# Dividing one pair's attention context by a second product's sums instead of dividing its weights first, with three small moves in the opening order

## The chip, the cores and the metric

One core of one Trainium2 chip runs the whole kernel. The time is the device time of one execution in microseconds (us); the time before is the median of three runs. The trace is of one further execution and counts from the start of its span.

## The reference, cut to what matters

`x` and `ctx_1024` are 128 batches of 128 tokens of 256 numbers, all in float32. One cross-attention block with 16 heads of 16 is followed by a feed-forward layer of 1024.

```python
q = heads(x @ Wq + bq); k = heads(ctx @ Wk + bk); v = heads(ctx @ Wv + bv)
scores = einsum('bhqd,bhkd->bhqk', q, k) / sqrt(16)
scores = where(j < i, scores, -1e30)        # query i, key j: strictly lower
attn = softmax(scores);  attn[:, :, 0, :] = 0
h = layer_norm(x + einsum('bhqk,bhkd->bhqd', attn, v) @ Wo + bo) * g1 + b1n
out = layer_norm(h + relu(h @ W1 + b1) @ W2 + b2) * g2 + b2n
```

## The kernel before

The 128 batches go through the core as 64 pairs, numbered p from 0. A pair's tokens are 256 columns of the transposed tiles `xT` and `cT`. `queries`, `keys` and `values` are products on TensorE; ScalarE (ACT) takes queries and keys out of PSUM with scale and bias. `values_out` copies the values into two tiles padded with zeros, `vz` and `vd`, and fills one half of `vd` with a DMA.

The scores of a pair come in two parts. `scores(p, 1)` has the queries 64 to 127 against 128 keys (2048 columns for the 16 heads), `scores(p, 0)` the queries 0 to 63 against 64 keys (1024 columns: the low scores). Both batches of the pair lie on the 128 partitions. For each part the softmax is a relay of four engines:

- `mask` on VectorE (DVE, L345): scores plus the mask, PSUM to the tile `sm`.
- `maximum`: a row maximum on DVE (L356), its subtraction on GpSimd (POOL, L357).
- `exponential` on ACT (L364).
- `sums`: row sums on DVE (L376), their reciprocals on DVE (L377), the multiplication of the weights by them on POOL (L378).

`ONE`, `TWO` and `ALL` are heads 0 to 7, 8 to 15, and all of them. The weights are then transposed to `pT`. In the steady stage this is done by DVE and by DMAs (`turn`, `bring`); for pairs 0, 1 and 63 it is done on TensorE, with ACT copying the transposes out of PSUM (`turn_on_pe`, L421 and L423). `weigh` multiplies `pT` with the values into one PSUM bank `pc` (96 small matmuls, L438 and L448). `context` copies `pc` into `cxT` on ACT (L460), leaving out token 0. `attention_out` (L467) applies Wo. `attention_sum`, `attention_stats` and `norm1` are DVE and POOL work that yields the normalised `x1`; for pair 0 `norm1` is L508, and TensorE transposes `x1` (L226, tile `ptn`).

Everything is under `manual_schedule` for all engines, so each engine runs its instructions in the order in which the program issues them. That order is written out by hand: first an opening for pairs 0 and 1, then `step(p)` for p = 2 to 62, then a closing for pair 63 and the rest. In `step`, pair 2 has branches of its own. TensorE's results go to PSUM tiles of two kinds: two tiles of two banks for scores (`pair`), and four single banks for everything else (`bank`).

The opening of before, where the change lies, runs in this order: transposes of pair 0, `bkh`, `bvw`, `bqs_c` (the query bias times the score scale), `queries(0)`, keys of pair 0, `scores(0, 1)`, transposes of pair 1, `values(0)`, the softmax of pair 0 mixed with `queries(1)`, `scores(0, 0)`, `keys(1)`, `values(1)`, `fold_values` and `scores(1, 1)`; then `turn_on_pe(0, ...)`, `scores(1, 0)`, `weigh(0)`, `context(0)`, `attention_out(0)`, with pair 1's softmax between them, and `queries(2)`, `keys(2)`, `values(2)`. Then `step(2)` begins with `scores(2, 1)`.

Of the kernel before, what the change touches and what calls it, by code (L numbers as in the profile page):

```python
# [8 lines left out]
F32 = mybir.dt.float32  # L9
# [4 lines left out]
P = 128  # L14
# [5 lines left out]
def tile_cross_attention_block(  # L20
# [178 lines left out]
    for i in range(2):  # L199
        vz = const.tile([P, 2, HH, 4, DK], F32, tag=f"vz{i}", name=f"vz{i}")  # L200
        nc.gpsimd.memset(vz, 0.0)
        vzs.append(vz)
        vd = const.tile([P, 2, HH, 2, DK], F32, tag=f"vd{i}", name=f"vd{i}")
        nc.gpsimd.memset(vd, 0.0)
        vds.append(vd)

    cxT = const.tile([P, KC, 2, P], F32, tag="cxT", name="cxT")
    nc.gpsimd.memset(cxT, 0.0)
# [4 lines left out]
    def bank(name):  # L213
        return ps_1.tile([P, 512], F32, tag="ps1", name=name)
# [137 lines left out]
    def maximum(p, hi, part):  # L352
        st = states[p]
        n = P if hi else HP
        sm, nmx = st["sm", hi], st["nmx", hi]
        nc.vector.tensor_reduce(nmx[:, part], sm[:, part, :], AX.X, ALU.max, negate=True)  # L356
        nc.gpsimd.tensor_tensor(  # L357
            sm[:, part, :], sm[:, part, :],
            nmx[:, part, None].to_broadcast([P, part.stop - part.start, n]), ALU.add,
        )  # L360

    def exponential(p, hi, part):
        sm = states[p]["sm", hi]
        nc.scalar.activation(sm[:, part, :], sm[:, part, :], AF.Exp)  # L364
# [3 lines left out]
    def sums(p, hi, part):  # L368

        st = states[p]  # L370
        sm = st["sm", hi]
        n = sm.shape[2]
        su = small.tile([P, H], F32, tag=f"su{hi}", name=f"su{hi}_{p}_{part.start}")
        rs = small.tile([P, H], F32, tag=f"rs{hi}", name=f"rs{hi}_{p}_{part.start}")
        su, rs = su[:, part], rs[:, part]
        nc.vector.tensor_reduce(su, sm[:, part, :], AX.X, ALU.add)  # L376
        nc.vector.reciprocal(rs, su)  # L377
        nc.gpsimd.tensor_tensor(  # L378
            sm[:, part, :], sm[:, part, :],
            rs[:, :, None].to_broadcast([P, part.stop - part.start, n]), ALU.mult,  # L380
        )
# [43 lines left out]
                pt.rearrange("p (n i a) -> p n i a", i=NS, a=32),  # L425
            )

    def weigh(p):

        st = states[p]  # L430
        pT = st.pop("pT")
        pc = bank(f"pc_{p}")

        for m in range(KC):
            for s in range(2):
                at = (m * 2 + s) * P
                for j in range(NS):
                    nc.tensor.matmul(  # L438
                        pc[32 * j : 32 * j + 32, at : at + HP],
                        st["vd"][:, s, 4 * m + j].rearrange("p e d -> p (e d)"),  # L440
                        pT[:, 2 * s : 2 * s + 2, H + 2 * j + m, :],
                        start=True, stop=True,
                    )
            for s in range(2):
                at = (m * 2 + s) * P
                for e in range(2):
                    for j in range(NS):
                        nc.tensor.matmul(  # L448
                            pc[32 * j : 32 * j + 32, at + HP : at + P],
                            st["vz"][:, s, 4 * m + j, 2 * e : 2 * e + 2, :].rearrange(  # L450
                                "p e d -> p (e d)"
                            ),
                            pT[:, 2 * s : 2 * s + 2, 4 * j + 2 * m + e, :],
                            start=(e == 0), stop=(e == 1),
                        )
        st["pc"] = pc

    def context(p):
        pc = states[p].pop("pc").rearrange("p (u i) -> p u i", i=P)
        nc.scalar.copy(cxT.rearrange("p m s i -> p (m s) i")[:, :, 1:], pc[:, :, 1:])  # L460

    def attention_out(p):
        st = states[p]
# [141 lines left out]
    def add_values(ps):  # L605
        nc.vector.scalar_tensor_tensor(bov_r, ps[:, :D], live, bo_r, ALU.mult, ALU.add)
# [78 lines left out]
    for which, first in (("x", tokens_of[0][:, 0:2]), ("c", c_first[:, 0:2])):  # L685
# [2 lines left out]
        pt = transposed(first, f"pt{which}_0")  # L688
        nc.vector.tensor_copy(st[which + "T"].rearrange("p k i -> p (k i)"), pt)  # L689

    bkh = const.tile([P, KC, 2], F32, tag="bkh", name="bkh")
    for m in range(KC):
        nc.vector.tensor_scalar(bkh[:, m, :], half, bk_c[:, m : m + 1], None, ALU.mult)

    bvw = const.tile([P, KC, P], F32, tag="bvw", name="bvw")
    nc.vector.tensor_copy(bvw, bv_c[:, :, None].to_broadcast([P, KC, P]))

    bqs_c = const.tile([P, KC], F32, tag="bqs_c", name="bqs_c")
    nc.vector.tensor_scalar(bqs_c, bq_c, QSCALE, None, ALU.mult)

    queries(0)

# [38 lines left out]
    mask(0, 0, 1)  # L741
    maximum(0, 0, ALL)
    exponential(0, 1, TWO)
    sums(0, 1, ONE)
    keys(1)
    sums(0, 1, TWO)
    exponential(0, 0, ALL)
    values(1)
    ps_bv = fold_values()
    sums(0, 0, ALL)  # L750
    scores(1, 1)
    mask(1, 1, 0)
    add_values(ps_bv)
    maximum(1, 1, ONE)
    turn_on_pe(0, 1, range(2))
    values_out(1)
    turn_on_pe(0, 1, range(2, 4))
    mask(1, 1, 1)
    maximum(1, 1, TWO)
    add_bo(0)  # L760
    turn_on_pe(0, 0, range(2))
    tokens(2, "x")
    scores(1, 0)
    exponential(1, 1, ONE)
    weigh(0)
    context(0)
    mask(1, 0, 0)
    mask(1, 0, 1)
    maximum(1, 0, ALL)
    tokens(2, "c")  # L770
    attention_out(0)
    exponential(1, 1, TWO)
    sums(1, 1, ONE)
    attention_sum(0)
    attention_stats(0)
    exponential(1, 0, ALL)
    queries(2)
    sums(1, 1, TWO)
    keys(2)
    norm1(0)  # L780
# [18 lines left out]
    def step(p):  # L799
        nonlocal waiting  # L800
        if p > 2:
            load_ahead(p)
        scores(p, 1)
        mask(p, 1, 0)
        maximum(p, 1, ONE)
        if p > 2:
            second(p - 3, 0)
            mask(p, 1, 1)
            maximum(p, 1, TWO)
            exponential(p, 1, ONE)  # L810
            second(p - 3, 1)
            if p + 2 < NP:
                tokens(p + 2, "c")
        else:
            turn_x1_on_pe(0)
            turn_on_pe(1, 1, range(2))
            fold_norm1()
            add_b1()
            hidden(0, range(FC // 2))
            mask(p, 1, 1)  # L820
            maximum(p, 1, TWO)
            exponential(p, 1, ONE)
            turn_on_pe(1, 1, range(2, 4))
            low_scores(p)
            hidden(0, range(FC // 2, 3 * FC // 4))
            turn_on_pe(1, 0, range(2))
            tokens(3, "x")
            add_bo(1)
        summed = []
        sums(p, 1, ONE)  # L830
        exponential(p, 1, TWO)
        if p > 2:
            second_sum(p - 3)
            summed = [p - 3]
        else:
            tokens(3, "c")
            load_ahead(2)
            load_tokens(2)
            exponential(p, 0, ALL)
        sums(p, 1, TWO)  # L840


        weigh(p - 1)
        context(p - 1)
        if p > 2:
            scores(p, 0)
        if p == 3:
            scale_w1()
            nc.gpsimd.tensor_tensor(b1e_c, b1e_c, b1_c, ALU.add)
        queries(p + 1)  # L850
        if p > 2:
            mask(p, 0, 0)
            mask(p, 0, 1)
            maximum(p, 0, ALL)
        if p > 2:
            exponential(p, 0, ALL)
        else:
            sums(p, 0, ALL)
            add_bo(2)
        turn(p, 1, 0)  # L860
        turn(p, 1, 1)
        for q in waiting:
            finish(q)
        attention_out(p - 1)
        attention_sum(p - 1)
        if p > 2:
            sums(p, 0, ALL)
        else:
            turn(p, 0, 0)
            bring(p, nc.sync, range(NS * NS // 2))  # L870
        attention_stats(p - 1)
        if p + 2 < NP:
            tokens(p + 2, "x")
            if p == 2:
                tokens(p + 2, "c")
        if p > 2:
            turn(p, 0, 0)
            bring(p, nc.sync, range(NS * NS // 2))
        keys(p + 1)
        norm1(p - 1)  # L880
        turn_x1(p - 1)
        values(p + 1)
        values_out(p + 1)
        for q in waiting:
            store(q)
        add_bo(p + 1)
        if p == 2:
            residual1(0)
        residual1(p - 1)
        for q in summed:  # L890
            stats(q, states[q]["t2"], 2)
        for q in summed:
            scale_and_shift(q)
        at = NS * NS // 2

        def share(f):
            nonlocal at
            n = NS * NS - at if f == FC - 2 else 0 if f == 0 or p == 2 else NS // 2
            bring(p, nc.scalar, range(at, at + n))
            at += n  # L900

        hidden(p - 2, range(0 if p > 2 else 3 * FC // 4, FC), share)
        for q in summed:
            norm2(q)
        waiting = summed
# [129 lines left out]
```

## Time and profile before

| what | value |
|---|---|
| median of three runs | 1587.98 us (1587.69 to 1590.0) |
| profiled execution, its own time | 1587.93 us |
| span of its trace | 1586.2 us |
| TensorE (PE) busy | 1572.0 us, 99% of the span |
| DVE busy | 1373.7 us, 87% |
| POOL busy | 1282.1 us, 81% |
| ACT busy | 756.7 us, 48% |
| granted TensorE clock | 1.0 |

The profiled execution lies 0.05 us below the median, and 1.73 us of it lie outside the span. A share of busy time is a mean over the opening, 61 steps and the closing. The change touches only the opening and step 2, so it is the first 75 us that have to be read instruction by instruction.

### The profile page before, as it was taken

What the parts mean: (1) busy time and instruction counts of PE and PEld (TensorE: products, weight loads), DVE (VectorE), ACT (ScalarE), POOL (GpSimd) and SP (SyncE); (2) the same over time, 40 slices, a digit from 0 to 9 for tenths busy, and PEclk for the clock granted to TensorE, in tenths of its full rate; (3) what the DMA queues carried; (4) which work ended last, traced back from release to release, by engine and by line L of the source; (5) the groups of instructions that cost most, each with busy time, mean ns of one, the idle gap of its engine ahead of it and who ended that gap; (6) DMA issues with size and microseconds to landing.
All of it is one profiled execution on the core that took longest, in us unless ns stands there. A gap on an engine that the chain in (4) does not pass through costs nothing.

```text
span 1586.2 us, 41271 instructions
## 1 busy us (share of the span) xinstructions
PE 1572.0 (99%) x16512; PEld 1329.7 (84%) x16512; DVE 1373.7 (87%) x1990; ACT 756.7 (48%) x1498; POOL 1282.1 (81%) x1104
## 2 busy tenths in 40 slices
PE   8999999999999999999999999999999999999998
PEld 6788888888888888888888888888888888888887
DVE  7999888888898888898898988888889888889872
ACT  5555445444444454454444544544444455445442
POOL 7888888788888888888888888888888888788883
PEclk9999999999999999999999999999999999999999
DMA  9555655655556556556556565565555655654521
GB/s 198 111 133 125 153 141 120 148 126 135 147 127 148 133 125 157 139 120 148 129 135 150 127 147 125 120 159 131 136 135 126 150 147 121 148 136 105 127 78 34
DMA packets 479935, 210.12 MB, mean 132 GB/s; under 512 B 348672, under 2 KB 448256, under 8 KB 479744
## 3 DMA queue, kind: packets, MB, share of 16 engines
q1 hardware_dynamic: 371104, 134.29, 38.4%
q10 hardware_dynamic: 108640, 73.19, 17.7%
q8 instruction: 131, 2.15, 0.6%
q14 instruction: 60, 0.49, 0.1%
HBM read 70.00 MB, written 33.03 MB: 65 GB/s over the span
## 4 chain that ended last, share of the span: by engine, by line
PE 95%; DMA 1%; DVE 1%; POOL 1%; issue 1%; SPq 0%; ACT 0%; ACTq 0%; POOLq 0%; DVEq 0%
PE ph L646 28%; PE py L664 27%; PE pq L260 7%; PE po L467 7%; PE pv L292 7%; PE pk L260 7%; PE pss L326 7%; PE pc L448 3%; PE pc L438 2%; DMA vd<-vz 0%; PE ptp L421 0%; POOL sm L378 0%; DMA x1t<-tbx 0%; DVE sm L345 0%; DMA c_first<-in_ctx_dram 0%
## 5 line engine op out<-in xcount | busy, mean ns | idle before, releaser
L357 POOL TENSOR_TENSOR sm<-sm,nmx 128x1024 f32<-128x1024 f32 x192 | 364.3, 1898 | 119.7 <-DVE nmx L356 119.4
L646 PE MATMUL ph<-x1T,w 128*128 128x256 f32 x2048 | 453.5, 380 | 0.3 <-DMA x1T<-x1t 0.3
L664 PE MATMUL py<-w,hT 128*128 128x256 f32 x2016 | 452.5, 383 | 0.0
L664 PEld LDWEIGHTS py<-w,hT 128*128 128x128 f32 x2016 | 378.8, 190 | 71.5 <-issue 15.0
L378 POOL TENSOR_TENSOR sm<-sm,rs 128x1024 f32<-128x1024 f32 x192 | 364.4, 1899 | 89.5 <-DVE rs L377 87.8
L646 PEld LDWEIGHTS ph<-x1T,w 128*128 128x128 f32 x2048 | 389.9, 191 | 52.9 <-DMA x1T<-x1t 0.6
L652 ACT ACTIVATE hT<-ph,b1e_c 128x256 f32<-128x256 f32 x504 | 208.4, 471 | 203.3 <-PE ph L646 103.1
L364 ACT ACTIVATE sm<-sm 128x1024 f32<-128x1024 f32 x192 | 201.4, 1054 | 206.3 <-POOL sm L357 205.7
L376 DVE TENSOR_REDUCE su<-sm 128x8 f32<-128x1024 f32 (+1 forms) x192 | 233.7, 1217 | 64.8 <-ACT sm L364 62.0
L345 DVE TENSOR_TENSOR sm<-pss,neg 128x1024 f32<-128x1024 f32 (+1 forms) x256 | 235.3, 940 | 51.5 <-PE pss L326 51.2
L391 DVE STREAM_TRANSPOSE tb<-sm 128x1024 f32<-128x1024 f32 x183 | 220.0, 1227 | 28.4 <-POOL sm L378 28.4
L356 DVE TENSOR_REDUCE nmx<-sm 128x8 f32<-128x1024 f32 (+1 forms) x192 | 234.2, 1220 | 6.6
L542 ACT ACTIVATE t<-t,nb,sd 128x256 f32<-128x256 f32 x124 | 67.7, 593 | 187.0 <-DMA pT<-tb 120.9
L260 PE MATMUL pq<-xT,wq 128*128 128x256 f32 x512 | 127.6, 392 | 0.3 <-DVE xT L689 0.3
L282 ACT ACTIVATE kT<-pk,bkh,half 128x256 f32<-128x256 f32 x252 | 120.6, 558 | 3.6 <-PE pk L260 3.6
L467 PE MATMUL po<-wo,cxT 128*128 128x256 f32 x512 | 121.1, 380 | 0.7 <-ACT cxT L460 0.7
L292 PE MATMUL pv<-wv,cT 128*128 128x256 f32 x512 | 121.0, 380 | 0.0
L260 PE MATMUL pk<-cT,wk 128*128 128x256 f32 x504 | 119.2, 380 | 0.0
L326 PE MATMUL pss<-kT,qT 32*64 32x256 f32 (+1 forms) x4096 | 116.4, 334 | 1.7 <-ACT kT L713 1.3
L271 ACT ACTIVATE qT<-pq,bqs_c 128x256 f32<-128x256 f32 x128 | 53.6, 469 | 121.5 <-PE pq L260 116.3
L260 PEld LDWEIGHTS pq<-xT,wq 128*128 128x128 f32 x512 | 92.4, 190 | 20.9 <-issue 10.3
L521 POOL TENSOR_TENSOR x1b<-x,g_r 128x512 f32<-128x512 f32 x64 | 81.7, 1277 | 34.8 <-DVE x L513 34.8
(93 smaller groups left out, 1764.1 us busy)
## 6 DMA issues: line engine op xcount, KB each, us to landing
pT<-tb SPq DMA_DIRECT2D x488, 96.0 KB, 2.9
pT<-tb ACTq DMA_DIRECT2D x488, 96.0 KB, 2.7
out_dram<-t ACTq DMA_DIRECT2D x63, 256.0 KB, 2.5
xb<-in_x_dram SPq DMA_DIRECT2D x124, 128.0 KB, 4.4
cb<-in_ctx_dram SPq DMA_DIRECT2D x124, 128.0 KB, 4.4
x<-in_x_dram SPq DMA_DIRECT2D x31, 512.0 KB, 5.5
x1t<-tbx SPq DMA_DIRECT2D x248, 64.0 KB, 2.3
x1T<-x1t SPq DMA_DIRECT2D x62, 256.0 KB, 3.2
```

Of the source, the lines that this page charges most:

```text
L260: nc.tensor.matmul(ps[:, m * TP : (m + 1) * TP], w[:, k, m * P : (m + 1) * P], src[:, k, :], start=(k == 0), stop=(k == KC - 1),)
L292: nc.tensor.matmul(pv[:, s * D : (s + 1) * D], st["cT"][:, k, s * P : (s + 1) * P], wv[:, k, :], start=(k == 0), stop=(k == KC - 1),)
L326: nc.tensor.matmul(sps[r // 2][s * HP : (s + 1) * HP, r % 2, m * 2 * n : (m + 1) * 2 * n].rearrange("p (e j) -> p e j", e=2), st["qT"][str ...
L345: nc.vector.tensor_tensor(st["sm", hi][:, part, :].rearrange("p (r n) j -> p r n j", r=2), st["sps", hi][t][:, :, : 4 * n].rearrange("p r ...
L356: nc.vector.tensor_reduce(nmx[:, part], sm[:, part, :], AX.X, ALU.max, negate=True)
L357: nc.gpsimd.tensor_tensor(sm[:, part, :], sm[:, part, :], nmx[:, part, None].to_broadcast([P, part.stop - part.start, n]), ALU.add,)
L376: nc.vector.tensor_reduce(su, sm[:, part, :], AX.X, ALU.add)
L378: nc.gpsimd.tensor_tensor(sm[:, part, :], sm[:, part, :], rs[:, :, None].to_broadcast([P, part.stop - part.start, n]), ALU.mult,)
L391: nc.vector.transpose(st["tb"][:, :, at : at + 256].rearrange("p j (n a) -> p n j a", a=32), st["sm", hi].rearrange("p h j -> p (h j)")[:, ...
L467: nc.tensor.matmul(po[:, s * D : (s + 1) * D], cxT[:, k, s, :], wo[:, k, :], start=(k == 0), stop=(k == KC - 1),)
L646: nc.tensor.matmul(ph[:, i * TP : (i + 1) * TP].rearrange("p (s i a) -> p s i a", s=2, a=32), w1[:, k, (f + i) * P : (f + i + 1) * P], st[ ...
L664: nc.tensor.matmul(st["py"][:, s * D : (s + 1) * D], st["hT"][:, f, s * P : (s + 1) * P], w2[:, f, :], start=(f == 0), stop=(f == FC - 1),)
```

## The change

Pair 0's weights are no longer divided by their sums: the three `sums(0, ...)` are gone. `weigh` is split into a shared body, `weighed`, and two callers. `weigh_ones(0)` runs the same 96 matmuls with ones (`oz`, `od`) in place of the padded values and so puts the sums of the weights into a second bank, `pd`, at the places where `pc` holds the context. `context(0)` then takes the reciprocal of `pd` and multiplies `pc` by it, both on DVE; the other pairs keep the copy on ACT. Six memsets on POOL fill the two tiles of ones.

`bqs_c` is made before `bkh` and `bvw`. In the opening `scores(1, 0)` goes behind `weigh(0)`, `maximum(1, 1, ONE)` and `add_values` behind `turn_on_pe(0, 1, ...)`, the two `exponential(1, 1, ...)` go ahead, and `attention_stats(0)` goes behind `queries(2)`. In step 2, which is the third, `low_scores(2)` is issued ahead of the second `turn_on_pe(1, 1, ...)`.

```diff
+    oz = const.tile([P, 2, 2, DK], F32, tag="oz", name="oz")
+    od = const.tile([P, 2, DK], F32, tag="od", name="od")
+    nc.gpsimd.memset(oz, 0.0)
+    nc.gpsimd.memset(od, 0.0)
+    for e in range(2):
+        nc.gpsimd.memset(oz[:, e, e], 1.0)
+        nc.gpsimd.memset(od[e * HP : (e + 1) * HP, e], 1.0)
...
-    def weigh(p):
-
-        st = states[p]
-        pT = st.pop("pT")
-        pc = bank(f"pc_{p}")
+    def weighed(pT, low, high, name):
+        pc = bank(name)
...
-                        st["vd"][:, s, 4 * m + j].rearrange("p e d -> p (e d)"),
+                        low(s, 4 * m + j).rearrange("p e d -> p (e d)"),
...
-                            st["vz"][:, s, 4 * m + j, 2 * e : 2 * e + 2, :].rearrange(
-                                "p e d -> p (e d)"
-                            ),
+                            high(s, 4 * m + j, e).rearrange("p e d -> p (e d)"),
...
+    def weigh_ones(p):
+
+        st = states[p]
+        st["pd"] = weighed(
+            st["pT"], lambda s, u: od, lambda s, u, e: oz[:, e], f"pd_{p}"
+        )
 
     def context(p):
-        pc = states[p].pop("pc").rearrange("p (u i) -> p u i", i=P)
-        nc.scalar.copy(cxT.rearrange("p m s i -> p (m s) i")[:, :, 1:], pc[:, :, 1:])
+        st = states[p]
+        pc = st.pop("pc").rearrange("p (u i) -> p u i", i=P)
+        to = cxT.rearrange("p m s i -> p (m s) i")[:, :, 1:]
+        if "pd" in st:
+            rd = small.tile([P, 2 * KC, P], F32, tag="rd", name=f"rd_{p}", bufs=1)
+            nc.vector.reciprocal(
+                rd[:, :, 1:], st.pop("pd").rearrange("p (u i) -> p u i", i=P)[:, :, 1:]
+            )
+            nc.vector.tensor_tensor(to, pc[:, :, 1:], rd[:, :, 1:], ALU.mult)
+        else:
+            nc.scalar.copy(to, pc[:, :, 1:])
...
+    bqs_c = const.tile([P, KC], F32, tag="bqs_c", name="bqs_c")
+    nc.vector.tensor_scalar(bqs_c, bq_c, QSCALE, None, ALU.mult)
+
     bkh = const.tile([P, KC, 2], F32, tag="bkh", name="bkh")
...
-    bqs_c = const.tile([P, KC], F32, tag="bqs_c", name="bqs_c")
-    nc.vector.tensor_scalar(bqs_c, bq_c, QSCALE, None, ALU.mult)
...
     exponential(0, 1, TWO)
-    sums(0, 1, ONE)
     keys(1)
-    sums(0, 1, TWO)
     exponential(0, 0, ALL)
     values(1)
     ps_bv = fold_values()
-    sums(0, 0, ALL)
+
+
     scores(1, 1)
     mask(1, 1, 0)
-    add_values(ps_bv)
-    maximum(1, 1, ONE)
     turn_on_pe(0, 1, range(2))
     values_out(1)
     turn_on_pe(0, 1, range(2, 4))
+    maximum(1, 1, ONE)
+    add_values(ps_bv)
     mask(1, 1, 1)
     maximum(1, 1, TWO)
     add_bo(0)
     turn_on_pe(0, 0, range(2))
+    exponential(1, 1, ONE)
     tokens(2, "x")
+    weigh_ones(0)
+    weigh(0)
     scores(1, 0)
-    exponential(1, 1, ONE)
-    weigh(0)
     context(0)
     mask(1, 0, 0)
     mask(1, 0, 1)
     maximum(1, 0, ALL)
+    exponential(1, 1, TWO)
     tokens(2, "c")
     attention_out(0)
-    exponential(1, 1, TWO)
     sums(1, 1, ONE)
     attention_sum(0)
-    attention_stats(0)
     exponential(1, 0, ALL)
     queries(2)
+    attention_stats(0)
     sums(1, 1, TWO)
     keys(2)
     norm1(0)
...
             exponential(p, 1, ONE)
+            low_scores(p)
             turn_on_pe(1, 1, range(2, 4))
-            low_scores(p)
             hidden(0, range(FC // 2, 3 * FC // 4))
```

More of the change, by code (lines that the diff above doesn't have):

```diff
@@ L455, in weigh @@
                         )
-        st["pc"] = pc
-    def context(p):
-        pc = states[p].pop("pc").rearrange("p (u i) -> p u i", i=P)
-        nc.scalar.copy(cxT.rearrange("p m s i -> p (m s) i")[:, :, 1:], pc[:, :, 1:])
+        return pc
+    def weigh(p):
+        st = states[p]
+        vz, vd = st["vz"], st["vd"]
+        st["pc"] = weighed(
+            st.pop("pT"), lambda s, u: vd[:, s, u],
+            lambda s, u, e: vz[:, s, u, 2 * e : 2 * e + 2, :], f"pc_{p}",
+        )
[4 more added lines that the diff above has]
+        )
+    def context(p):
+        st = states[p]
+        pc = st.pop("pc").rearrange("p (u i) -> p u i", i=P)
[4 more added lines that the diff above has]
+                rd[:, :, 1:], st.pop("pd").rearrange("p (u i) -> p u i", i=P)[:, :, 1:]
+            )
+            nc.vector.tensor_tensor(to, pc[:, :, 1:], rd[:, :, 1:], ALU.mult)
+        else:
+            nc.scalar.copy(to, pc[:, :, 1:])
     def attention_out(p):
```

## The prediction

> **What bounds the kernel now.** I read the page first, then the waits of PE up to 75 us, then busy time by stage, and last the timeline of the opening.
>
> ```profile
> PE 1572.0 (99%) x16512; PEld 1329.7 (84%) x16512; DVE 1373.7 (87%) x1990; ACT 756.7 (48%) x1498; POOL 1282.1 (81%) x1104
> PE 95%; DMA 1%; DVE 1%; POOL 1%; issue 1%; SPq 0%; ACT 0%; ACTq 0%; POOLq 0%; DVEq 0%
> ```
>
> PE is busy 99% of the span and carries 95% of the chain that ended last. From about 73 us to the closing it has next to no waits (0.7 us), so a shift of PE at the end of the opening arrives at the end of the kernel unchanged. The whole question is when PE passes the end of the opening.
>
> ```profile
> PE ptp L421 <- POOL sm L378: 2.5, 3, 0.9
> PE pss L326 <- ACT kT L713: 1.3, 1, 1.3
> PE pc L438 <- DMA x1t<-tbx: 0.8, 1, 0.8
> PE pc L438 <- ACT pT L423: 0.7, 2, 0.5
> PE po L467 <- ACT cxT L460: 0.7, 1, 0.7
> PE ptn L226 <- DVE x L508: 0.2, 1, 0.2
> ```
>
> These waits of PE (us in total, times, longest) are what the change can win: 6.2 us in all. The first is pair 0's transposes waiting for POOL's division.
>
> ```profile
> 20.00:30.00 10.00, 7.53 (x163) 5.69 (x165) 9.45 (x13) 7.67 (x15) 9.73 (x6) 1.00 1.05 288
> 30.00:40.00 10.00, 9.14 (x109) 7.18 (x98) 9.72 (x16) 6.12 (x13) 9.21 (x7) 1.00 0.89 124
> ```
>
> The columns are the length, then PE, PEld, DVE, ACT and POOL busy. From 20 to 40 us DVE is the busiest but for POOL in the first row, and from 30 to 40 it has 0.28 us of idle time. It is a second bound beside PE: the last wait in the list above, ptn for L508, says that at 40 us PE still waits for DVE.
>
> ```profile
> 8.79 0.17 DVE L699 TENSOR_SCALAR bqs_c<-bq_c 128x2 f32<-128x2 f32 x1
> 9.06 0.84 ACT L271 ACTIVATE qT<-pq,bqs_c 128x256 f32<-128x256 f32 x2 [5.24 <-DMA g_c<-in_L_xattn_ln_g_dram]
> 9.61 0.99 DVE L718 TENSOR_SCALAR kT<-pk,half,bkh 128x256 f32<-128x256 f32 x2 [0.65 <-PE pk L707]
> 10.86 1.12 PE L326 MATMUL pss<-kT,qT 32*64 32x256 f32 x32 [1.29 <-ACT kT L713]
> 23.59 1.09 PE L421 MATMUL ptp<-ident,sm 128*128 128x128 f32 x8 [0.94 <-POOL sm L378]
> 24.28 1.07 ACT L423 COPY pT<-ptp 128x512 f32<-128x512 f32 x2 [1.51 <-PE ptp L421]
> 26.88 2.19 ACT L423 COPY pT<-ptp 128x512 f32<-128x512 f32 x4
> 29.83 1.25 DVE L345 TENSOR_TENSOR sm<-pss,neg 128x512 f32<-128x512 f32 x2
> 34.28 0.67 DVE L493 TENSOR_TENSOR t<-po,xb 128x512 f32<-128x512 f32 x1
> 37.44 2.52 DVE L508 SCALAR_TENSOR_TENSOR x<-t,mv,sd 128x256 f32<-128x256 f32 x2
> ```
>
> Start, length, engine. The reader should see that the bias at 8.79 holds back qT, that ACT's six pT copies end at 29.07, and that DVE's low mask of pair 1 (29.83) leads without a break to norm1 (ends 39.96), after which PE goes on at 40.02.
>
> **The change part by part.** The sum is a new timetable of the opening, in the profiled execution's own times.
>
> *Query bias first.* bqs_c no longer stands behind bvw on DVE. Its input was issued ahead of bk_c's, which had landed when bkh ran at 6.68, so it is ready by about 6.9. qT then starts when its product ends (the eight pq matmuls run from 5.85 to 7.84), at 7.9 instead of 9.06, and ACT's kT half is done at 9.8. The other kT half is DVE's and ends at 10.60 as before, so the second half of the scores can start at 10.65 and takes 0.53 to 0.59: pss ends at 11.24, not 11.98. That is -0.74, not the 1.16 that qT gains. PE runs without a gap from there to the end of scores(1, 1), so it passes on: transposes could start at 22.85.
>
> *No division before the transposes.* Three sums leave DVE (3 x 1.2 + 0.65 = 4.25 us) and three L378 leave POOL (5.6 us). The transposes then follow scores(1, 1), whose slot is 1.05 long, at 20.79 + 1.05 = 21.84. ACT's string from its first pT copy to the sixth is back to back in before (24.28 to 29.07, 4.79 us, with values_out in between), so it keeps its length: from 21.84 + 0.69 = 22.53 to 27.32. That is 1.75 earlier, of which 0.74 is the bias. Three of PE's waits are gone, but half of their room is lost to ACT's string.
>
> *Second product.* weigh_ones has weigh's 96 matmuls, 28.95 to 30.66, so 1.69 between starts: pd is done at 29.05. Meanwhile DVE has finished max(1, 1, TWO) and tokens(2) by 27.7, and then waits for pd for 1.4 us, with pair 1's low mask behind it.
>
> *Reciprocal and multiplication.* They sit on DVE between pd and everything that leads to norm1. No row shows a reciprocal of 508 columns. The near rows are these:
>
> ```profile
> L377 DVE RECIPROCAL rs<-su 128x8 f32<-128x8 f32 x10 | 2.0, 203 | 0.5
> L377 DVE RECIPROCAL rs<-su 128x16 f32<-128x16 f32 x4 | 1.0, 253 | 0.1
> ```
>
> Eight more columns cost 50 ns, 6.3 to 6.4 ns each. Carried to 508 columns: 203 + 500 x 6.4 = 3.40 us. [...] From below, an ordinary pass over 512 columns out of PSUM takes 0.67 (L493). I take 3.4, because the two rows are the same instruction[...]. The multiplication is of L493's kind: 0.67.
>
> So the reciprocal runs from 29.12 to 32.52, the product to 33.2, and the low mask starts at 33.14 instead of 29.83: **+3.31 for DVE**. [...] DVE's load over the opening hardly changes (4.25 out, 4.07 in); what changes is the place. The sums were done early, while other engines supplied DVE with work; the reciprocal comes late and behind a wait.
>
> *Who is late next.* attention_out needs the product, so it starts at 33.25, not 31.34. Four products of 1.73 bring PE to 40.2. kT of pair 2 now waits on ACT behind exp(1, 0), which moves with the low mask: the POOL subtraction ends at 37.6, exp at 38.7, qT at 39.5, kT at 41.35, so scores(2, 1) ends at about 42.0. All that is hidden: DVE's string from the low mask to norm1 (29.83 to 39.96) has no slack to give back, so norm1 ends at 43.27 and PE goes on at 43.33 instead of 40.02: **+3.3 on PE**. The second L508 takes 2.1 of its 2.5 us while POOL runs L378 beside it; the order there is unchanged, so I move it whole.
>
> *scores(1, 0) behind weigh.* It ends at 29.05 + 1.69 + 0.7 = 31.45. The reciprocal covers it; were that free, the low mask would still start at 31.5, 1.7 late.
>
> *Low scores sooner.* In step 2 this takes PE's scores past eight transposes (0.97 us). It issues no DMA, and passes nothing on POOL or SP; ACT's copies of these transposes wait for an exponential till 48.0 anyway. DVE gets its low mask 0.9 earlier, so turn(2, 0) comes 0.9 sooner. What it could win is the 0.8 us for which weigh(2) waits for the pT transfers. But SP's third pT issue stands still until 65.16, when a transfer lands that ACT issued after its hT of PE's own hidden product. That follows PE, not DVE. I count 0, between 0 and -0.8.
>
> *At nothing.* Six memsets on POOL, about 0.15 each: POOL idles 7.94 us before 14.62; without that cover, 0.9. attention_stats (DVE, POOL) passes exp and queries (ACT, PE): no shared queue. add_values and max pass turn_on_pe: DVE against PE and ACT. The new pd is one more tile for the four single banks. If the third transpose is given pv's bank, it waits for values_out (25.2) rather than for a copy, about +0.8; in before it did not. I count 0.
>
> The sum: 1587.93 + 3.3 = 1591.2, and 3.2 above the median, which is 0.05 higher. 0.2% is 3.18 us, about what a measurement of this kernel can tell from no change.
>
> **The rivals.** *The reciprocal costs like any other pass (0.7 us).* Then scores(1, 0) sets the low mask: +1.7, 1589.6, or 1588.8 with the 0.8 of weigh(2). It decides below about 1.7 us, 3 ns a column. For it: nothing in the rows; against it: 6.4 ns from the same instruction. This ends as no change.
>
> [...]
>
> *A bank holds the transposes back:* +0.8 on the forecast, 1592.0. Against it: four banks, and at 25.44 two transposes started before pv was read out.
>
> *Low scores give weigh(2)'s wait back:* -0.8, 1590.4, no change by the bound.
>
> *A gain above 0.2%* would take 3.2 of the 6.2 us of waits, with 1.69 of new matmuls on PE itself; even with the DVE work free, attention_out starts at 31.5 against 31.34. Only if norm1 did not bound PE at all could it come near.
>
> **How the numbers follow.** Forecast as worked out 0.4 (centre 1591.2, the bound at 1587.98 + 3.18 = 1591.16), [...]a bank or another late buffer 0.1, weigh(2)'s wait given back 0.12, cheap reciprocal 0.14, a gain 0.04. Slower: 0.24 of the 0.4, 0.2 and 0.1, together 0.54; within: the other 0.16, 0.12 and 0.14, together 0.42; faster 0.04. [...] The forecast's own range is 1590.4 to 1592.2.
>
> **What would show it.** Right: a RECIPROCAL of 128x508 near 3.4 us that starts about 1.4 us after DVE's last work; ptp at about 21.9 without a POOL wait; po waiting some 1.8 us for DVE; ptn waiting about 1.3 us for L508; the gap at weigh(2) as it was. Wrong: a reciprocal under 1.7 us, pT copies that end after 28, or a norm1 that ends before 41.

## The result and the profile after

| | before | after |
|---|---|---|
| median | 1588.61 us (1587.69 to 1590.0, six runs) | 1595.0 us (1594.23 to 1596.29, six runs) |
| profiled execution, its own time | 1587.93 us | 1594.36 us |
| span of its trace | 1586.2 us | 1592.6 us |

The ratio is 1.0039, interval 1.0028 to 1.0049: slower, by 6.4 us between the medians. The forecast was 1591.2 with a range to 1593.0. Its direction held; its size did not.

First the waits of TensorE up to 80 us in the kernel after (us in total, times, longest):

```profile
PE pc L443 <- issue: 3.7, 2, 3.1
PE warm L711 <- POOL ident masks.py:199: 1.4, 1, 1.4
PE pd L443 <- ACT pT L431: 0.8, 1, 0.8
PE pc L443 <- ACT pT L431: 0.7, 2, 0.5
PE ptp L429 <- DVE bov_r L634: 0.6, 1, 0.6
PE ptn L234 <- DVE x L536: 0.4, 1, 0.4
```

The three waits for POOL's division are gone, as worked out. At the head stands an entry that the list of before did not have: TensorE stood still in `weigh(0)` for "issue", that is, for nothing that the profile shows as awaited. That is 3.06 of the 3.7 us; the other 0.6 are at `weigh(2)`, where before had 0.8 put down to a transfer. The timelines of TensorE and VectorE show what it does (start, length, engine):

```profile
22.72 1.09 PE L429 MATMUL ptp<-ident,sm 128*128 128x128 f32 x8
27.69 0.75 PE L443 MATMUL pd<-pT,od 128*32 128x64 f32 x14 [0.80 <-ACT pT L431]
30.07 0.23 PE L443 MATMUL pc<-pT,vd 128*32 128x64 f32 x2
33.36 0.36 PE L443 MATMUL pc<-pT,vd 128*32 128x64 f32 x10 [3.06 <-issue]
34.16 0.98 PE L334 MATMUL pss<-kT,qT 32*64 32x128 f32 x32
35.07 3.34 PE L495 MATMUL po<-wo,cxT 128*128 128x256 f32 x8
45.32 0.55 PE L234 MATMUL ptn<-ident,x 128*128 128x128 f32 x3 [0.42 <-DVE x L536]
```

```profile
29.66 3.33 DVE L483 RECIPROCAL rd<-pd 128x508 f32<-128x508 f32 x1 [0.92 <-PE pd L453]
34.33 0.69 DVE L486 TENSOR_TENSOR cxT<-pc,rd 128x508 f32<-128x508 f32 x1 [1.33 <-PE pc L453]
35.16 1.29 DVE L353 TENSOR_TENSOR sm<-pss,neg 128x512 f32<-128x512 f32 x2
42.75 2.52 DVE L536 SCALAR_TENSOR_TENSOR x<-t,mv,sd 128x256 f32<-128x256 f32 x2
```

The reciprocal lasts 3.33 us, against 3.40 forecast, and it ends at 32.99. But the multiplication then waits 1.33 us for the product with the values, because TensorE stood still in the middle of it, between 30.07 and 33.36. TensorE also runs slower behind the stop. These are stretches of that time (length, then PE, PEld, DVE, ACT and POOL busy, granted clock, DMA share, GB/s):

```profile
30.00:33.40 3.40, 0.34 (x27) 0.17 (x18) 3.00 (x1) 1.06 (x1) 1.33 (x2) 1.00 1.31 135
33.40:35.00 1.60, 1.60 (x76) 1.24 (x76) 0.67 (x1) 0.00 (x0) 0.00 (x0) 0.82 1.00 133
35.00:37.00 2.00, 2.00 (x13) 1.57 (x6) 1.82 (x4) 0.00 (x0) 0.00 (x0) 0.50 0.86 123
37.00:38.40 1.40, 1.40 (x6) 1.17 (x5) 1.40 (x3) 0.00 (x0) 0.61 (x1) 0.70 0.30 91
38.40:40.00 1.60, 1.60 (x10) 1.39 (x9) 1.57 (x3) 0.28 (x1) 1.48 (x2) 1.00 0.29 90
```

Behind the idle stretch of 3.06 us the granted clock reads 0.82 and then 0.50: Wo's products (`po`) take 3.34 us, where the same eight took 2.00 before, at a clock of 1.00:

```profile
31.34 2.00 PE L467 MATMUL po<-wo,cxT 128*128 128x256 f32 x8 [0.68 <-ACT cxT L460]
```

What was TensorE waiting for? The queues of the page have a row that is in no step of the prediction; the second line is the same row in the DMA view of 30.0 to 31.6 us alone (packets, MB, share of the engines):

```profile
q8 instruction: 132, 2.16, 0.6%
```

```profile
q8 instruction: 1, 0.02, 5.9%
```

132 packets of 2.16 MB are about 16.4 KB each. The kernel after has 16608 matmuls and as many weight loads, 33216 in all, and the trace also records 582 instructions of TensorE's own sequencer (semaphores and the like): 33798, or 256.0 for each packet. In before, 33024 and 584 over 131 packets are 256.5. From these counts I take it that q8 brings TensorE its instructions, 256 to a packet on average. One such packet begins at 30.06 us and takes 1.52: TensorE starts its last matmul at 30.08 and goes on 3.3 us after the packet began, 1.8 after it ended. Whether that is the cause is what the experiments were for.

### The profile page after: what moved, and what is told of

It reads as the page before. It is cut to its first block, busy times and chain, and to the rows that moved or that the text cites. A ratio compares the mean times of both kernels' runs of the same rounds, so it can differ in the third digit from the quotient of the medians.

```text
span 1592.6 us, 41457 instructions
## 1 busy us (share of the span) xinstructions
PE 1577.4 (99%) x16608; PEld 1329.8 (83%) x16608; DVE 1374.0 (86%) x1986; ACT 755.7 (47%) x1497; POOL 1275.9 (80%) x1107
## 3 DMA queue, kind: packets, MB, share of 16 engines
q8 instruction: 132, 2.16, 0.6%
## 4 chain that ended last, share of the span: by engine, by line
PE 96%; DMA 1%; SPq 1%; DVE 1%; issue 0%; ACT 0%; POOL 0%; POOLq 0%; ACTq 0%; DVEq 0%
PE py L692 28%; PE ph L674 28%; PE pq L268 7%; PE po L495 7%; PE pk L268 7%; PE pv L300 7%; PE pss L334 6%; PE pc L453 4%; PE pc L443 2%; SPq L93 1%; DMA w<-in_L_xattn_W_dram 0%; DMA x<-in_x_dram 0%; PE ptp L429 0%; DMA pT<-tb 0%; DMA cb<-in_ctx_dram 0%
## 5 line engine op out<-in xcount | busy, mean ns | idle before, releaser
L386 POOL TENSOR_TENSOR sm<-sm,rs 128x1024 f32<-128x1024 f32 x189 | 358.9, 1899 | 91.2 <-DVE rs L385 87.3
L384 DVE TENSOR_REDUCE su<-sm 128x8 f32<-128x1024 f32 x189 | 230.1, 1217 | 66.2 <-ACT sm L372 63.4
L495 PEld LDWEIGHTS po<-wo,cxT 128*128 128x128 f32 x512 | 98.2, 192 | 13.9 <-DVE cxT L486 0.3
## 6 DMA issues: line engine op xcount, KB each, us to landing
out_dram<-t ACTq DMA_DIRECT2D x63, 256.0 KB, 2.5
x1T<-x1t SPq DMA_DIRECT2D x62, 256.0 KB, 3.2
```

Of the source, the lines that this page charges most:

```text
L386: nc.gpsimd.tensor_tensor(sm[:, part, :], sm[:, part, :], rs[:, :, None].to_broadcast([P, part.stop - part.start, n]), ALU.mult,)
L495: nc.tensor.matmul(po[:, s * D : (s + 1) * D], cxT[:, k, s, :], wo[:, k, :], start=(k == 0), stop=(k == KC - 1),)
```

## The experiments

The first theory is the instruction supply: the second product puts 192 very short TensorE instructions (loads and matmuls) ahead of a block that is not there yet. The rival is DVE: the reciprocal and the multiplication delay what follows, as the prediction has it, and the stop only happens in their shade. Below, n counts TensorE's recorded instructions from the start: its loads and matmuls, and its sequencer's own (9 or 10 of the first 705 where there is a stop).

### The parts by themselves

**e1: the same kernel without the slow reciprocal.** A copy takes its place.

```diff
-            nc.vector.reciprocal(
+            nc.vector.tensor_copy(
```

> The changed kernel with the reciprocal left out: an ordinary copy of the sums out of PSUM stands in its place, so the context is multiplied by the sums, not divided. Instruction theory: TensorE stopped in the first pair's second product because its next block of instructions had not come; the stop stays at the same place (after about 705 loads and matmuls) and lasts about 3 us, attention_out starts near 34.5 instead of 35.07, and the time is at most 1 us below the changed kernel (594 to 595 over a thousand). Reciprocal theory: the stop, which began 0.4 us after the reciprocal began and ended 0.4 us after it ended, is caused by it; then there is no stop, attention_out starts near 32, and the time is 3 to 4 us below the changed kernel, near 1591.5.

Measured: 1596.47 us, ratio 1.0043 (1.0028 to 1.0058). Timeline, TensorE and VectorE:

```profile
29.41 0.69 DVE L483 COPY rd<-pd 128x508 f32<-128x508 f32 x1 [0.92 <-PE pd L453]
33.47 0.52 PE L443 MATMUL pc<-pT,vd 128*32 128x64 f32 x10 [3.42 <-issue]
35.05 0.69 DVE L486 TENSOR_TENSOR cxT<-pc,rd 128x508 f32<-128x508 f32 x1 [4.95 <-PE pc L453]
```

Taking 2.64 us out of DVE brings nothing: the stop stays where it was, and the multiplication waits 4.95 us for `pc` instead of 1.33. In the kernel as it is, the reciprocal does not set the end: DVE alone is not the answer.

**e2: the ones in fewer, wider matmuls.** 24 matmuls of 128 columns make the same sums as 48 of 64 (the trace has each twice). The first of its two loops:

```diff
-        st["pd"] = weighed(
-            st["pT"], lambda s, u: od, lambda s, u, e: oz[:, e], f"pd_{p}"
-        )
+        pT = st["pT"]
+        pd = st["pd"] = bank(f"pd_{p}")
+        for s in range(2):
+            for j in range(NS):
+                to = pd[32 * j : 32 * j + 32, :].rearrange("p (m s i) -> p s m i", m=KC, s=2)[:, s]
+                nc.tensor.matmul(
+                    to[:, :, :HP].rearrange("p m (i a) -> p m i a", a=32),
+                    od.rearrange("p e d -> p (e d)"),
+                    pT[:, 2 * s : 2 * s + 2, H + 2 * j : H + 2 * j + 2, :].rearrange(
+                        "p i m a -> p m i a"
+                    ),
+                    start=True, stop=True,
+                )
...
```

> The changed kernel with the product with ones in 12 wide matmuls of 128 columns in place of 48 of 64: same sums, fewer instructions. Instruction theory: about 144 loads and matmuls fewer lie before the end of the block, so TensorE reaches it about at the end of scores(1, 0), where it waits for the division anyway; no stop inside the second product, attention_out near 33.5 at full clock, time 2 to 3 us below the changed kernel. Reciprocal theory: TensorE still stops from 0.4 us after the reciprocal starts until 0.4 us after it ends, attention_out near 35, time as the changed kernel.

Measured: 1595.07 us, 1.0036 (1.0025 to 1.0048); 96 loads and matmuls fewer, not the 144 I had expected. The stop did not shrink, it moved to another product:

```profile
31.05 0.43 PE L334 MATMUL pss<-kT,qT 32*64 32x128 f32 x4
34.70 1.08 PE L334 MATMUL pss<-kT,qT 32*64 32x128 f32 x28 [3.22 <-DVE cxT L508]
```

These scores do not read `cxT`, whose multiplication ended at 33.99; the releaser in the bracket is inferred, and wrong here. The stop is now inside `scores(1, 0)`, but at the same count: n = 705, as in after and in e1. A stop that stays with the count and not with the operation is what the first theory says.

**e3 and e4: the two edits that can stand alone.** The bias first, and the low scores sooner, each put into the kernel before.

```diff
+    bqs_c = const.tile([P, KC], F32, tag="bqs_c", name="bqs_c")
+    nc.vector.tensor_scalar(bqs_c, bq_c, QSCALE, None, ALU.mult)
+
     bkh = const.tile([P, KC, 2], F32, tag="bkh", name="bkh")
```

> The kernel before with the scaled query bias made first, nothing else. The prediction's step: scores(0, 1) end 0.74 us earlier (11.24 instead of 11.98) and so does the kernel: -0.7 us. Rival: the first products' own pace (in the trace of the changed kernel the first eight pq matmuls took 2.44 instead of 1.99 us) varies from execution to execution and covers it: no difference that the runs can tell from zero, 0 within 1 us.

```diff
-            turn_on_pe(1, 1, range(2, 4))
             low_scores(p)
+            turn_on_pe(1, 1, range(2, 4))
```

> The kernel before with the low scores sooner in step 2, nothing else. The prediction's step: DVE's low mask of pair 2 about 0.9 us earlier, the wait of weigh(2) between 0 and 0.8 us, so 0 to -0.8 us. Rival: the order of instructions shifts the ends of TensorE's instruction blocks in the steps and with them small stops there, up to 1 us either way.

Measured: e3 1589.09 us, 1.0001 (0.9992 to 1.001); e4 1588.75, 0.9996 (0.9988 to 1.0005). Neither can be told from nothing, though e3's interval also holds the -0.74 of the forecast, and e4's the -0.8 that the forecast gave as its end. For the bias, e3's timeline says more:

```profile
6.19 2.33 PE L260 MATMUL pq<-xT,wq 128*128 128x256 f32 x8
8.56 0.84 ACT L271 ACTIVATE qT<-pq,bqs_c 128x256 f32<-128x256 f32 x2 [4.74 <-PE pq L260]
10.49 0.69 PE L326 MATMUL pss<-kT,qT 32*64 32x256 f32 x16 [0.25 <-ACT kT L713]
11.34 0.69 PE L326 MATMUL pss<-kT,qT 32*64 32x256 f32 x16 [0.15 <-DVE kT L718]
```

The bias is no longer what qT waits for, and the gap of 1.29 us ahead of the scores is 0.25 and 0.15. But the first products ran slower than in the trace of before: pq lasts 2.33 against 1.99 there and ends at 8.52 against 7.84. `scores(1, 1)` then starts at 21.58, against 21.53 before. In e4, pq took 2.10 without the bias edit: the speed of these first products differs from trace to trace, from 1.99 us (before, e1) to 2.67 (e2); the same kind of eight takes 1.89 later on (at 14.57 in before). The granted clock from 6 to 8 us reads 1.00 in before, after and e3, whose lengths are 1.99, 2.44 and 2.33; what sets the pace these traces do not show.

### The stop

**f1 and f2: fewer transfers at that time.** The loads of `w2` and of pairs 1 and 2's further tokens are issued at about 47 us instead of in the opening, in the kernel after (f1) and before (f2).

```diff
-    w2 = weight(W2, "w2")
-    load_tokens(1)
-    load([4, 5])
...
+            w2 = weight(W2, "w2")
+            load_tokens(1)
+            load([4, 5])
```

> The changed kernel with three loads (w2, the tokens of group 1, the blocks of pairs 4 and 5; 2.5 MB) issued behind add_b1 in step 2, near 47 us, instead of near 21 us. Theory of the late block: TensorE stopped at load or matmul 705 because the transfer that brings its next 16 KB of instructions stood behind these loads; with them gone the block comes in time, the stop of 3.1 us shrinks to under 1 us, the clock stays up, attention_out starts near 33.7, and the time falls by 2 to 3 us to about 1592.5. Rival, block on demand: the block is only asked for when the queue runs dry and takes 3 us whatever else is moved; the stop stays at 705 and at about 3 us, time as the changed kernel.

> The kernel before with the same three loads issued late. Control: in before TensorE does not stop at its block's end in the opening, so both theories expect no change there, within 0.5 us of before; a change would be the loads' own.

Measured: f1 1601.83 us, 1.0081 (1.0066 to 1.0096); f2 1598.71, 1.006 (1.0043 to 1.0077). Both totals are spoilt by one new wait that comes with the moved loads in step 2, 8.1 us in f1 and 7.7 in f2; between the two medians lie 3.1 us (waits of TensorE, 60 to 110 us, f1):

```profile
PE pc L440 <- DMA x1t<-tbx: 8.1, 1, 8.1
```

The opening ahead of it can still be read. f1's timeline:

```profile
28.94 3.33 DVE L480 RECIPROCAL rd<-pd 128x508 f32<-128x508 f32 x1 [0.92 <-PE pd L450]
30.81 0.36 PE L440 MATMUL pc<-pT,vd 128*32 128x64 f32 x10 [1.23 <-issue]
33.15 1.99 PE L492 MATMUL po<-wo,cxT 128*128 128x256 f32 x8 [0.86 <-DVE cxT L483]
43.16 0.55 PE L231 MATMUL ptn<-ident,x 128*128 128x128 f32 x3 [0.99 <-DVE x L533]
```

With the DMA engines nearly idle (share 0.06 from 28 to 29 us, where after has 1.33) the packet begins at 28.43 and takes 0.93 us, and the stop, at n = 705 again, is 1.23 us instead of 3.06. That is not under 1 us, as the theory of the late block had it, nor the 3 us of its rival. It fits beneath the reciprocal: po waits for DVE, its length is 1.99 (the granted clock reads 1.00 from 31 to 37 us), and TensorE passes ptn at 43.16, 2.9 us behind f2's 40.30. This is the timetable of the prediction, which had +3.3.

**f6: f1 with e1's copy.** The edit is the two above together.

> The late loads kernel with the reciprocal left out (a plain copy of the sums in its place, so the context is multiplied, not divided). If the stop is gone there, this shows what the reciprocal itself costs once nothing hides it: the prediction had the low mask at 33.14 with it and 31.5 without, so about 1.6 us below the late loads kernel. If the stop is still there, no difference between the two.

Measured: 1601.12 us, 1.0077 (1.0062 to 1.0092). ptn is passed at 42.79, 0.4 us before f1, not the larger gain that I had put down. A stop of 1.45 us remains at n = 705, so even here the reciprocal is mostly covered by the stop.

**f4: the second product alone.** Before with `weigh_ones(0)` ahead of `weigh(0)`; its result is not read, and the division stays where it was.

```diff
+    weigh_ones(0)
     weigh(0)
```

> The kernel before with the product with ones run ahead of weigh(0) and its result read by nobody; the weights are divided as before. Priced as the prediction did, by TensorE's time alone: +1.7 us. Theory of the instruction block: 192 short instructions pull load or matmul 705 forward into weigh(0), TensorE stops there for about 3 us and then runs at half clock for a while: +5 to +6 us, nearly all that the changed kernel lost, without any of its DVE work or moves.

Measured: 1596.1 us, 1.0046 (1.0031 to 1.0061), so +6.8 us between the medians, with none of the DVE work and none of the moves. TensorE:

```profile
33.88 0.59 PE L453 MATMUL pc<-pT,vz 128*32 128x64 f32 x27 [2.49 <-issue]
36.06 3.78 PE L486 MATMUL po<-wo,cxT 128*128 128x256 f32 x8 [0.68 <-ACT cxT L479]
39.63 2.91 PE L268 MATMUL pq<-xT,wq 128*128 128x256 f32 x8
46.98 0.66 PE L234 MATMUL ptn<-ident,x 128*128 128x128 f32 x4
```

ptn comes at 46.98, 6.96 us later than before. The parts are 1.7 for the matmuls, 2.5 for the stop, 1.8 for po (3.78 against 2.00) and 1.0 for pq (2.91 against 1.89), 7.0 together (its scores(1, 1) also began 0.5 later, at 22.03, so half a us of these lay beside other waits). This is the sequence by itself: the product, the stop at n = 705, and half a clock behind it (granted 0.50 from 36 to 40 us).

**g3: everything but the second product.** After without `weigh_ones(0)`; the context is copied on ACT.

```diff
-    weigh_ones(0)
```

> The changed kernel without the product with ones: the first pair's context is copied by ACT as in before and stays undivided, so the division is left out altogether. It shows what the other moves are worth. By the instruction theory TensorE reaches instruction 705 behind scores(1, 0) as in before, so no long stop; by the prediction's timetable attention_out starts near 30.7 to 31 but pair 1's low mask, with scores(1, 0) behind weigh, at about 31.3 instead of 29.83, so TensorE gains nothing at the transposes of x1: within 1.5 us of before, either side. If taking POOL's division out of the way is worth what TensorE waited for it, 2.5 us faster than before.

Measured: 1589.35 us, 0.9999 (0.999 to 1.0007). No stop. The gain that the missing division and the moves might have brought is not there either:

```profile
29.79 1.97 PE L495 MATMUL po<-wo,cxT 128*128 128x256 f32 x8 [0.15 <-ACT cxT L488]
39.88 0.55 PE L234 MATMUL ptn<-ident,x 128*128 128x128 f32 x3 [0.99 <-DVE x L536]
```

po starts 1.55 us earlier than before (29.79 against 31.34), and at ptn 0.14 of it is left: TensorE waits 0.99 us for DVE's norm1. Its string starts with the low mask at 29.71, against 29.83 before, because scores(1, 0) now stands behind `weigh(0)`. The moves and the missing division together thus bring nothing that these runs can tell from zero, and with f4 the loss is the product with ones and what it sets off.

**g1, g4 and g2: shift the count.** With 84 more TensorE instructions early on, the 705th stands 84 sooner in the program. If that number alone stops TensorE, it stops there, still in `weigh(0)`; if the block was on its way and came late, it may now come in time. Two of the twelve warm-up transposes are replaced by 22 one-column products, in after (g1) and before (g4); g2 is g1 with scores(1, 0) ahead of the two products.

```diff
-    for i in range(12):
+    for i in range(10):
...
+    for i in range(22):
+        nc.tensor.matmul(warm[:32, i : i + 1], ident[:, :32], ident[:, :1], start=True, stop=True)
```

> The changed kernel with 84 more TensorE instructions in the warm-up: two of its twelve warm transposes replaced by 22 products of one column, read by nobody. Theory of the late block: blocks hold 256 instructions[...], the block is there in time, and TensorE does not stop in the second product; attention_out starts near 33.5, TensorE passes the first transpose of x1 about 3 us later than in before, and the time is 1591.5 to 1592.5. If it is the number 705 that stops TensorE, whatever stands there (block on demand), it stops for about 3 us 84 instructions sooner, near 29.5, and the time stays near 1595.

> The kernel before with the same 84 instructions in the warm-up. Control: neither theory expects a stop here in the opening; within 0.5 us of before.

> The changed kernel with the 84 instructions in the warm-up, scores(1, 0) ahead of both products as in before, and its two masks on DVE ahead of the division, where DVE stood idle for pd. If the rest of the loss beyond the stop is DVE's string from the low mask to norm1, this gives back about 1 us of it: 1590.5 to 1591.5, still not below before. If that string does not matter, the same time as the shifted kernel.

Measured: g1 1594.97 us, 1.0036 (1.0023 to 1.0049); g4 1595.42, 1.004 (1.0025 to 1.0055); g2 1594.41, 1.0031 (1.002 to 1.0042). g1's stop is gone: instruction 706 follows the 705th within 0.04 us, so the number alone does not stop TensorE. But the packet began at 29.01 and n = 484, against 30.06 and n = 701 in after; how far ahead a block is asked for the runs do not show. TensorE waits for the division instead:

```profile
3.77 2.51 PE L713 MATMUL warm<-ident 128*32 128x1 f32 x44
33.03 0.66 PE L453 MATMUL pc<-pT,vz 128*32 128x64 f32 x30
36.61 2.47 PE L495 MATMUL po<-wo,cxT 128*128 128x256 f32 x8 [2.29 <-DVE cxT L486]
```

From the start of scores(1, 1) to ptn takes 22.04 us in g1 (24.41 to 46.45), against 22.54 in the forecast's timetable (20.79 to 43.33) and 23.65 in after (21.67 to 45.32). The remedy does not pay, though: the added products hold the opening up, scores(1, 1) starting at 24.41 instead of 21.67, and 25.19 in the control g4. The control was expected within half a us of before and lost 5.5 between the medians; its trace has 2.7 us of waiting for a transfer in step 2 as well, where before has 0.8. So g1 shows that the stop can go, but its total against g4 cannot say what the stop costs. In g2 the low mask comes at 31.05 instead of 36.47, and from scores(1, 1) to ptn it still takes 22.20 us (24.06 to 46.26); its median, 0.6 below g1's, is within the noise of the two.

The counts of all the traces side by side (us; n at which the second q8 packet began, times of instructions 705 and 706, and how long after the packet's begin and end the 706th came, from the traces' records):

```
kernel  packet began  ended  at n   705th   706th   after begin  after end
before         31.75  33.21   672   35.12   35.33          3.58       2.12
g3             29.94  31.45   669   33.54   33.75          3.81       2.30
g1             29.01  30.01   484   32.20   32.24          3.23       2.23
e4             31.94  33.41   674   35.07   35.28          3.34       1.87
e3             30.50  32.03   666   35.17   35.38          4.88       3.35
f2             29.49  30.73   494   35.41   35.62          6.13       4.89
g4             31.39  32.93   482   34.57   34.75          3.36       1.82
g2             25.37  26.74   448   31.44   31.44          6.07       4.70
after          30.06  31.58   701   30.08   33.36          3.30       1.78  stop
e1             30.43  31.98   705   29.83   33.47          3.04       1.49  stop
e2             31.66  33.17   705   31.22   34.71          3.05       1.54  stop
f4             30.82  32.33   654   31.18   33.89          3.07       1.56  stop
f1             28.43  29.36   572   29.36   30.81          2.38       1.45  stop
f6             28.53  29.74   581   29.41   31.07          2.54       1.33  stop
```

In the six traces with a stop TensorE runs up to the 705th instruction, whatever it is, and goes on 2.4 to 3.3 us after the packet began and 1.3 to 1.8 us after it ended. Where there is no stop, instruction 706 is reached later than that anyway, 1.8 to 4.9 us after the packet's end. Before is only 0.3 us beyond the slowest of the stops, and nothing in its waits tells of it. What fills the time between the packet's end and TensorE's start the traces do not show.

## Why the prediction was wrong

**The step that failed is "Second product".** It gave the product 1.69 us, its time on TensorE, and nothing else; that TensorE can stand still at a count of instructions was in no step and in no rival. The stop of 3.06 us came with the product: f4 has one too, of 2.49 us, and g3, without the product, has none. Its cost on the path is smaller, some 1.5 us, because the reciprocal runs beside it. From the forecast's low mask on DVE at 33.14 to the 35.16 of the trace there are 2.02 us:

- pd ready late, the reciprocal starting at 29.66 instead of 29.12: +0.54
- reciprocal 3.33 instead of 3.40: -0.07
- DVE's wait for `pc`: +1.34
- from the start of the multiplication to the mask 0.83 instead of 0.62: +0.21, scores(1, 0) now following the stop at a clock of 0.82

From the mask on, DVE's string has the length that was forecast (35.16 to 45.27, 10.11 us; 10.13 in before), so ptn is 1.99 late too: 45.32 against 43.33, and +5.3 against before instead of +3.3. The slow po of 3.34 us costs nothing more there, as DVE is busy without a break until it needs it.

**"Query bias first" fell short as well, by a term that it took over unchanged.** It should have given 0.74; scores(1, 1) starts at 21.67, not 20.79. The step kept the first products' pace of before. But the eight pq products ended at 8.62 instead of 7.84, and that is 0.78 of the 0.88. The edit itself does what the step says: in every trace that has it, scores(1, 1) starts 13.05 to 13.06 us after these products end (8.62 and 21.67 here, 8.02 and 21.08 in g3), where before needs 13.69 (7.84 and 21.53). Where the products end late, though, the bias has long been there and there is nothing to gain: f2, without the edit, has 13.05 too (8.77 and 21.82). Of the 0.88 us, 0.54 are left in the first term above. Why the pace differs is not settled.

**What held.** *Reciprocal:* the two small rows of the trace (6.4 ns a column) were right, 3.33 us measured. A longer one, on which 0.2 of the weight for "slower" and the upper end of the range, 1593.0, rested, was the author's assumption; no run shows it. *DVE's string as the second bound:* in f1, where the stop fits beneath the reciprocal, TensorE loses 2.9 us against f2, close to the 3.3 forecast; in g1, without a stop, scores(1, 1) to ptn takes 22.04 us against the 22.54 of the forecast. *No division before the transposes:* they start without a wait for POOL, 22.72, the forecast's 21.84 and 0.88. ACT's copies end at 28.03, the forecast's 27.32 and 0.71; with that one of the prediction's three signs of being wrong came true, copies that end after 28, by the late start and not by a bank. *At nothing:* the third transposes did wait 0.59 us, by the inferred releaser for the bank of `ps_bv` and not, as the rival had it, for pv's; g3, which has no `pd`, waits as long. It cost nothing, being hidden in ACT's string. *Low scores sooner:* nothing that e4 could tell from 0, as counted. *Not seen:* po's wait of 1.8 us for DVE, since TensorE itself was late; ptn waited 0.42 us for norm1 instead of 1.3.

**What lies beyond the opening.** The profiled execution took 3.2 us more than the forecast; 2.0 of that are the terms above, 1.2 come later. Set side by side by instruction, TensorE of after is 5.1 us behind before at 75 us and 6.35 at the end. The difference comes mostly in stops of 0.1 to 0.8 us scattered over the steps. Over the period of a step (24.26 us) these sum to 1.5 us in before and 3.3 in after, but to 2.0, 4.8, 4.0 and 3.1 in e3, e4, f2 and g3, which do not have the product. That they belong to the change is thus not shown; how much of the 6.4 us they are in the medians stays open. Some of them are the stop of the opening over again, in before too. The longest of before and that of e4, in which the releaser is "issue" once more, are these:

```profile
947.83 0.43 PE L326 MATMUL pss<-kT,qT 32*64 32x128 f32 x4 [0.40 <-issue]
950.30 0.43 PE L326 MATMUL pss<-kT,qT 32*64 32x128 f32 x4 [1.19 <-issue]
```

Both stand behind n = 20417, which is 705 + 77 x 256, and so do those of f2 and g3; TensorE goes on 1.4 to 1.7 us after the end of a q8 packet. In after one of 0.6 us from start to start stands behind 10689, 705 + 39 x 256.

## What to carry to other kernels

A block of very short instructions can have a price that its busy time does not hold: the product with ones was busy for 1.7 us, and TensorE then stood still for 3.06 us (2.49 in f4) behind the same count of instructions, 705. So when a change adds many of them, look at the queue rows of kind "instruction", and count the instructions to a packet, here 256 recorded ones on average; a gap at such a count, 705 or a multiple of 256 behind it here, with "issue" as its releaser, or with a releaser that the instruction does not read, is the sign. And before pricing a stall, follow it to the next engine: 3.06 us of stop cost some 1.5 here, since 3.33 us of reciprocal ran beside it, and taking the reciprocal away brought nothing for the same reason.

## What the hardware showed beyond that

- TensorE stopped at the same instruction count, n = 705, in six kernels in which different products stand there, and the later stops named above, in kernels with the product and without, lie whole multiples of 256 behind it. What starts the packet is open: it began at counts from 448 to 705 in the table.
- In g1 the granted clock read 0.85 and then 0.50 behind a wait of 2.29 us that ended at 36.61:

```profile
36.60:38.60 2.00, 1.99 (x8) 1.74 (x9) 1.97 (x3) 0.00 (x0) 0.00 (x0) 0.85 1.02 160
38.60:40.60 2.00, 2.00 (x7) 1.56 (x6) 2.00 (x3) 0.00 (x0) 1.52 (x1) 0.50 0.71 121
```

  Behind the stops of 2.49 to 3.42 us in f4, after, e2 and e1 it read 0.50 as well; behind f1's of 1.23 us it read 1.00 up to 37 us.

- The 44 one-column matmuls of g1's warm-up take 2.44 us from start to the next product (3.77 to 6.21), 55 ns each; those of `weigh_ones` have 64 columns and 1.7 us for 96, 18 ns each. Few columns did not make them cheap at that place, where the first products run slowly too.
